# A gated recurrence on one core: the inner level of the input products is divided by pairs of PSUM quadrants

## The chip, the cores and the metric

The kernel runs on one core of one Trainium2 chip. The metric is device time in microseconds (us) for one execution of the whole program. Engines are named as in the profile: PE (TensorE matmul), PEld (its weight loads), DVE (VectorE), ACT (ScalarE), POOL (GpSimd), SP (SyncE, which issues the DMAs).

## What is computed

A gated recurrent layer runs over 512 time steps for a batch of 8, with 512 inputs and 512 hidden units in float32, and its states are added to the input:

```
fused = sigmoid(concat([x_t, h]) @ w_W + w_b)
hidden_state, output_state = split(fused, 2)
memory_state = x_t @ wx_W + wx_b + hidden_state * (h @ wh_W + wh_b)
h_new = output_state * h + (1 - output_state) * tanh(memory_state)
out = x + hs            # hs: all 512 states
```

Two kinds of matrix products occur. Those with `h` depend on the step before. Those with `x_t` do not, and can be made ahead for many steps at once.

## The kernel before

**Steps.** The loop over `i` goes through T = 512 steps. All engines follow an order written out by hand (`tc.manual_schedule()`). A chunk is TC = 16 steps, a group is GS = 4 steps (`g, s = divmod(i, GS)`), and w is the place of a step in its chunk (0 to 15).

In each step PE first makes the products with `h`, in the order `A0 A1 A2 A3 D0 D1 D2 D3 H2 H3`. The digit is the quarter k of the contraction, and each entry is four matmuls, one for each quadrant j of 32 PSUM partitions. A0 and A1 write 256 columns of bank A, A2 and A3 write 192, D 128, H 64. A0, A1 need the first half of the state (`hT[0]`), A2, A3 the second (`hT[1]`). A float32 matmul appears in the trace as two MATMUL records and two weight loads. All of them are recorded at line L196, the helper `mm`.

Behind these, PE gets some of the products with `x` for the chunk after this one (`take(later, 3)`, or 4 in the last step of a chunk).

DVE and ACT turn the sums of step i into the new state. In DVE's order: `tr`, `md1A` and `tz` are 32x32 block transposes out of bank A (L534, L549); two scans `m<-md0A,md1A` (L522, `memory(0, .)`) read the two SBUF tiles md0A and md1A; transposes of A, D and H; two scans `hT<-hd0A,hT` (`update(0, .)`, first half of the new state); two scans `m<-md0B,md1B`; two transposes of `sz`; two scans `hT<-hd0B,hT` (`update(1, .)`, second half). ACT makes the sigmoids and tanhs between them. Behind the last scan stand DVE's jobs that no state waits for: `drain` (L398), transposes of `xs` (`turn_x`, L292) and two small memsets. Then comes `tr` of the next step, which waits for PE's bank A.

POOL begins each step's work with `ot<-xin,hT` (L686), the sum of x and the new state, and then does the jobs that are listed for that step: `for job, *args in jobs.get(i, ())`.

**Products with x.** For chunks 2 to 31 they are made by a fast scheme with two levels: seven outer products p, each made of seven inner products q. The inner level goes through `STAGES = (2, 5, 3, 1, 6, 7, 4)`. In each stage the seven outer products lie in two PSUM banks (`xps`), three in bank 0 (288 columns) and four in bank 1 (384 columns). One unit of work is one outer product: four matmuls of 96 columns, one for each quadrant. That is 49 units a chunk: three a step, four in step 15. A `drain` adds a bank to a tile in SBUF: stages 2, 5, 3 into `ee`, stages 1, 6, 7, 4 into `ff`. There are 14 drains a chunk, at most one a step.

**POOL's jobs.** The operands for the fast scheme come from sums of x on POOL: `x_sums`, 16 jobs for each chunk, two a step at w = 3 to 10. The outer sums are `result(e, n)`, seven jobs of 192 columns for e = 0 (from `ff[0]`, listed from w = 11) and seven for e = 1 (from `ff[1]`, from w = 15), two a step:

```python
        for e, w in ((0, 11), (1, 15)):
            for m, n in enumerate((0, 3, 2, 4, 1, 5, 6)):
                at_step(w0 + w + m // 2, (result, e, n))
```

They write `xs[0..3]`, one for each group of four steps, from which ACT (`spread`) and DVE (`turn_x`) fill banks and operands one group ahead.

Of the kernel before, what the change touches and what calls it, by code (L numbers as in the profile page):

```python
# [46 lines left out]
COLS = slice(64, 448)  # L47
# [7 lines left out]
def tile_cond_rnn_residual(  # L55
# [38 lines left out]
    nc = tc.nc  # L94
# [4 lines left out]
    const = ctx.enter_context(tc.tile_pool(name="const", bufs=1))  # L99
# [11 lines left out]
    bias = head[:, :512]  # L111
# [21 lines left out]
    wx = const.tile([P, NQ, NQ, 384], F32, name="wx")  # L133
# [40 lines left out]
    idle = const.tile([P, IDLE], F32, name="idle")  # L174

    tw = const.tile([P, 4, 2, NQ, HALF], F32, name="tw")
    ti = const.tile([P, 7, 4, NQ, BL], F32, name="ti")
    so = [const.tile([P, 4, 2, 2, 32], F32, name=f"so{q}") for q in range(2)]
    si = [const.tile([P, 7, 4, 32], F32, name=f"si{q}") for q in range(2)]
    off = [const.tile([P, 7, BL], F32, name=f"off{b}") for b in range(2)]  # L180
    ee = [const.tile([P, 7, BL], F32, name=f"ee{n}") for n in range(3)]
    ff = [const.tile([P, 7, 2, BL], F32, name=f"ff{n}") for n in range(2)]
    xs = [const.tile([P, 576], F32, name=f"xs{n}") for n in range(4)]

    def state(hf, i, slot=2):
# [7 lines left out]
    xps = [psum.tile([P, 512], F32, name=f"xp{q}") for q in range(2)]  # L193

    def mm(out_, lhsT, rhs, start=False):
        nc.tensor.matmul(  # L196
            out_, lhsT, rhs, start=start, stop=False, skip_group_check=True
        )
# [32 lines left out]
    def wx_of(kh, nh):  # L231
        return wx[:, 2 * kh : 2 * kh + 2, :, HALF * nh : HALF * nh + HALF]
# [5 lines left out]
    for t_ in xs[1:] + xs[:1]:  # L238
        nc.gpsimd.tensor_copy(t_[:, 64:128], bias[:, :64])
        nc.gpsimd.tensor_copy(t_[:, 512:], bias[:, 448:])  # L240
    for b in range(2):
        c0 = COLS.start + BL * b
        nc.gpsimd.tensor_copy(off[b][:, 0], bias[:, c0 : c0 + BL])
        nc.gpsimd.tensor_tensor(
            off[b][:, 6], bias[:, c0 + HALF : c0 + HALF + BL], bias[:, c0 : c0 + BL], ALU.subtract
        )
    for hf in range(2):
        for slot in (0, 2):
# [45 lines left out]
    def inner_weight(n, p, j=slice(0, NQ)):  # L294

        def w(k, b):
            c0 = slice(BL * b, BL * b + BL)
            if p < 2:
                return wx[:, 2 * p + k, j, c0]
            if p == 2:  # L300
                return wx[:, 2 + k, j, HALF + BL * b : HALF + BL * b + BL]
            return tw[:, p - 3, k, j, c0]

        a, b = [
            (w(0, 1), w(0, 0)),
            (w(1, 1), ti[:, p, 0, j]),
            (w(1, 1), w(0, 1)),
            (w(1, 0), ti[:, p, 1, j]),
        ][n]
# [36 lines left out]
    def x_sums(c):  # L346
        jobs = [(x_sum, c, n) for n in range(4)]
        return jobs + [(inner_x, c, n, p) for n in range(4) for p in (0, 2, 3)]

    def left(c, p, q):  # L350

        xr, kh = {1: (0, 0), 2: (0, 1), 4: (1, 1)}.get(p, (None, None))
        at = {1: 0, 2: 1, 4: 2, 5: 3, 6: 4, 7: 5, 3: 6}[p]
        if q in (3, 5, 6, 7):
            return si[c % 2][:, at, {5: 0, 6: 1, 7: 2, 3: 3}[q]]
        e, k = {1: (0, 0), 2: (0, 1), 4: (1, 1)}[q]
        if xr is None:
            return so[c % 2][:, at - 3, e, k]
        return x_block(c, xr, kh)[:, e, k]

    def right(p, q, j):

        kh, nh = {1: (0, 0), 2: (1, 0), 3: (1, 1)}.get(p, (None, None))
# [4 lines left out]
        w = tw[:, at - 3] if kh is None else wx_of(kh, nh)  # L368
        return w[:, k, j, BL * b : BL * b + BL]

    def products(c):

        for q in STAGES:
            for bank in range(2):
                for n, p in enumerate(SLOTS[bank]):
                    for j in range(NQ):
                        mm(
                            xps[bank][32 * j : 32 * j + 32, BL * n : BL * n + BL],
                            left(c, p, q),
                            right(p, q, j),  # L380
                            start=q in FRESH and n == 0,
                        )
                    yield

    def drain(q, bank):

        at, n = (slice(0, 3), 3) if bank == 0 else (slice(3, 7), 4)
        to, with_ = {
            2: (ee[0], off[0]),
            5: (ee[1], off[1]),  # L390
            3: (ee[2], off[1]),
            1: (ff[0][:, :, 0], ee[0]),
            6: (ff[0][:, :, 1], ee[2]),
            7: (ff[1][:, :, 1], ee[1]),
            4: (ff[1][:, :, 0], off[0]),
        }[q]
        src = xps[bank][:, : BL * n].rearrange("p (n b) -> p n b", n=n)
        nc.vector.tensor_tensor(to[:, at], src, with_[:, at], ALU.add)  # L398

    def result(e, n):  # L400

        f = [ff[e][:, v].rearrange("p b c -> p (b c)") for v in range(7)]
# [10 lines left out]
        nc.gpsimd.tensor_tensor(to, a, b, ALU.add)  # L413
# [38 lines left out]
    def at_step(i, *todo):  # L452
        jobs.setdefault(i, []).extend(todo)

    halves = [(n, p, h) for n in (0, 2, 1, 3) for p in range(7) for h in range(2) if n or p > 4]
    for at in range(0, len(halves), 3):
        for n, p, h in halves[at : at + 3]:
            todo = late.setdefault(at // 3, [])
            if h and todo and todo[-1][:2] == (n, p):
                todo[-1] = (n, p, slice(0, 4))  # L460
            else:
                todo.append((n, p, slice(2 * h, 2 * h + 2)))
    drains = {}
    for c in range(2, NCH):
        w0 = TC * c - LEAD
        for n, q in enumerate(x_sums(c)):
            at_step(w0 - (13 if c > 2 else 10) + n // 2, q)
        done = 0
        for w in range(TC):
            n = done  # L470
            done += 3 + w // 15
            for m, q in enumerate(STAGES):
                for bank in range(2):
                    if n < 7 * m + 3 + 4 * bank <= done:
                        drains.setdefault(w0 + w, []).append((q, bank))
        for e, w in ((0, 11), (1, 15)):
            for m, n in enumerate((0, 3, 2, 4, 1, 5, 6)):
                at_step(w0 + w + m // 2, (result, e, n))

    pool_done = {}  # L480
    for i in range(T):
        g, s = divmod(i, GS)
        c, t = divmod(i, TC)
        ps = banks[g % 2]
        if c > 0 and t in (1, 4, 7, 10):
            e, k = divmod(t // 3, 2)
# [5 lines left out]
        for n in (ORDER if i else FIRST).split():  # L492
            if n == "x":
# [153 lines left out]
        for d in drains.get(i, ()):  # L647
            drain(*d)
# [121 lines left out]
```

## Time and profile before

| | |
|---|---|
| three runs | 1629.16, 1630.44, 1631.74 us (median 1630.44) |
| profiled execution | 1634.49 us, of which the profiled span is 1632.7 us |
| granted TensorE clock | 1.0 |
| PE busy | 1622.7 us (99% of the span) |
| DVE / ACT / POOL busy | 1411.5 (86%) / 977.0 (60%) / 541.9 us (33%) |
| MATMUL records | 53291 |

The median of the three runs is 4 us below the profiled execution. Busy PE time counts a matmul from its start to its modelled end, and matmuls overlap, so the 99% do not say that PE has no time to spare.

### The profile page before, as it was taken

How to read it: one execution, taken by the hardware profiler on the slowest of the kernel's cores; microseconds unless marked ns; L12 is line 12 of the kernel's file. 1: busy time of each engine (PE TensorE's matmuls, PEld its weight loads, DVE VectorE, ACT ScalarE, POOL GpSimd, SP SyncE). 2: the span in 40 equal slices, each digit the busy share in tenths (PEclk: the TensorE clock that was granted, in tenths of full speed). 3: DMA queues.
4: the chain of work that ended last, by engine and by line, in shares of the span. 5: the costliest groups of instructions: out<-in, count | busy, mean ns of one | idle time of the engine just before them, and what ended most of it. 6: DMA issues, size and time to landing. Idle time of an engine off the chain costs nothing.

```text
span 1632.7 us, 126805 instructions
## 1 busy us (share of the span) xinstructions
PE 1622.7 (99%) x53291; PEld 1372.3 (84%) x53291; DVE 1411.5 (86%) x11757; ACT 977.0 (60%) x5521; POOL 541.9 (33%) x1443
## 2 busy tenths in 40 slices
PE   9999999999999999999999999999999999999998
PEld 6888888888888888888888888888888888888886
DVE  8988888888888888888888888888888888888887
ACT  4665666656666666566556566666665666665665
POOL 2333333333333333333333333333333333333320
PEclk9999999999999999999999999999999999999999
DMA  4000000000000000000000000000000000000000
GB/s 191 12 14 18 16 14 13 18 15 16 15 18 13 15 16 17 15 13 14 18 16 15 13 17 15 16 15 18 13 15 16 18 15 13 15 18 10 10 10 10
DMA packets 37437, 31.47 MB, mean 19 GB/s; under 512 B 4096, under 2 KB 35200, under 8 KB 36864
## 3 DMA queue, kind: packets, MB, share of 16 engines
q1 hardware_dynamic: 36864, 23.36, 4.6%
q8 instruction: 416, 6.82, 1.7%
q14 instruction: 157, 1.29, 0.3%
HBM read 14.96 MB, written 8.39 MB: 14 GB/s over the span
## 4 chain that ended last, share of the span: by engine, by line
PE 98%; DVE 1%; issue 0%; DVEq 0%
PE A L196 49%; PE D L196 27%; PE xp L196 16%; PE H L196 7%; DVE tr L534 0%; DVE m L522 0%; DVE md1B L592 0%; DVE hT L522 0%; DVE md1A L549 0%; DVE tz L534 0%; DVE md1B L549 0%; DVE zeros L163 0%; DVE hd0B L585 0%; DVE idle L557 0%; DVE ot L667 0%
## 5 line engine op out<-in xcount | busy, mean ns | idle before, releaser
L196 PE MATMUL A<-wa,hT 128*32 128x256 f32 x16352 | 882.5, 355 | 4.1 <-DVE hT L522 4.0
L196 PEld LDWEIGHTS A<-wa,hT 128*32 128x32 f32 x16352 | 512.0, 123 | 223.2 <-DVE hT L522 127.7
L196 PE MATMUL D<-wd,hT 128*32 128x128 f32 x16384 | 544.9, 273 | 0.0
L196 PEld LDWEIGHTS D<-wd,hT 128*32 128x32 f32 x16384 | 485.2, 122 | 19.6 <-DMA wd<-in_wd_dram 0.2
L686 POOL TENSOR_TENSOR ot<-xin,hT 128x32 f32<-128x32 f32 x503 | 134.5, 267 | 1041.7 <-DVE hT L522 957.8
L258 ACT ACTIVATE hT<-m 128x8 f32<-128x8 f32 x2048 | 323.9, 207 | 94.5 <-DVE m L522 93.7
L258 ACT ACTIVATE md0A<-tr 128x16 f32<-128x16 f32 x512 | 112.9, 221 | 389.9 <-DVE tr L534 389.9
L534 DVE STREAM_TRANSPOSE tr<-A 128x64 f32<-128x64 f32 x511 | 127.7, 250 | 205.4 <-PE A L196 204.7
L258 ACT ACTIVATE hT<-hT 128x16 f32<-128x16 f32 x1024 | 232.2, 227 | 92.0 <-DVE hT L522 85.3
L196 PE MATMUL H<-wa,hT 128*32 128x64 f32 x8208 | 212.3, 219 | 0.0
L196 PEld LDWEIGHTS H<-wa,hT 128*32 128x32 f32 x8208 | 189.6, 122 | 0.0
L522 DVE TENSOR_TENSOR_SCAN hT<-hd0A,hT 128x24 f32<-128x24 f32 x1024 | 172.7, 169 | 0.0
L522 DVE TENSOR_TENSOR_SCAN hT<-hd0B,hT 128x24 f32<-128x24 f32 x1024 | 171.9, 208 | 0.8 <-DVE hT L522 0.8
L522 DVE TENSOR_TENSOR_SCAN m<-md0B,md1B 128x24 f32<-128x24 f32 x1024 | 154.7, 193 | 0.4 <-issue 0.4
L196 PE MATMUL xp<-ti,si 128*32 128x96 f32 x5040 | 150.6, 246 | 0.0
L585 DVE STREAM_TRANSPOSE hd0B<-sz 128x32 f32<-128x32 f32 x1024 | 149.1, 191 | 0.0
L522 DVE TENSOR_TENSOR_SCAN m<-md0A,md1A 128x16 f32<-128x16 f32 x1024 | 143.8, 182 | 5.0
L413 POOL TENSOR_TENSOR xs<-ff 128x192 f32<-128x192 f32 x240 | 140.8, 597 | 4.7
L258 ACT ACTIVATE md0B<-tr 128x16 f32<-128x16 f32 x512 | 116.3, 227 | 41.8 <-DVE tr L534 1.2
L592 DVE STREAM_TRANSPOSE md1B<-A 128x64 f32<-128x64 f32 x511 | 130.0, 254 | 0.0
L258 ACT ACTIVATE hd0A<-tz 128x16 f32<-128x16 f32 x512 | 116.4, 227 | 21.5
L549 DVE STREAM_TRANSPOSE md1B<-H 128x64 f32<-128x64 f32 x512 | 128.3, 251 | 0.0
(109 smaller groups left out, 1906.0 us busy)
## 6 DMA issues: line engine op xcount, KB each, us to landing
out_dram<-ot SPq DMA_DIRECT2D x128, 64.0 KB, 1.7
xin<-in_x_dram SPq DMA_DIRECT2D x112, 64.0 KB, 2.5
wx<-in_wx_dram SPq DMA_DIRECT2D x4, 768.0 KB, 7.9
wa<-in_wa_dram SPq DMA_DIRECT2D x4, 512.0 KB, 11.5
wd<-in_wd_dram SPq DMA_DIRECT2D x1, 768.0 KB, 11.4
xin<-in_x_dram SPq DMA_DIRECT2D x2, 256.0 KB, 8.2
head<-in_xh_dram SPq DMA_DIRECT2D x1, 400.0 KB, 3.0
xin<-in_x_dram SPq DMA_DIRECT2D x3, 128.0 KB, 8.7
```

The costliest lines, as they stand in the source:

```text
L196: nc.tensor.matmul(out_, lhsT, rhs, start=start, stop=False, skip_group_check=True)
L258: inst = nc.scalar.activation(out_, in_, func, **kw).ins
L413: nc.gpsimd.tensor_tensor(to, a, b, ALU.add)
L522: return nc.vector.tensor_tensor_scan(*[t_[:, :, c_].rearrange("p n c s -> p (n c s)") for t_ in (out_, d0, d1)], 0.0, ALU.mult, ALU.add,).ins
L534: inst = nc.vector.transpose(t_.rearrange("p c n -> p (c n)"), raw[n][hf]).ins
L549: inst = nc.vector.transpose(md1[hf][g % 2][:, :, :, hf].rearrange("p n c -> p c n"), raw["h"][hf]).ins
L585: nc.vector.transpose(hd0[1][i % 2][:, :, q, 2], sz[:, 32 * q : 32 * q + 32]).ins
L592: nc.vector.transpose(md1[1][g % 2][:, :, :, 0].rearrange("p n c -> p c n"), ps["A"][:, :HU])
L686: pool_done[i + 1] = nc.gpsimd.tensor_tensor(ot[:, t], x_of(c, slice(0, NQ), t, 1), hTs[(i + 1) % NH][:, :, :, B * s1 : B * s1 + B, 2].rea ...
```

## The change

In a stage, the seven outer products no longer take one column block each over all four quadrants. Two products now share 192 columns: one uses quadrants 0 and 1, the other quadrants 2 and 3 (`PASS`). Passes A, B (bank 0, now 384 columns) and C (bank 1, now 288 columns) hold two products each. Pass D holds the seventh alone, 96 columns wide. A unit is still four matmuls of 96 columns, but `deal` hands PE as many units of one pass as it still may in this step, in one group of four matmuls. A step with three units becomes two groups (192 and 96 columns), 8 matmuls in place of 12; the step with four units becomes two groups of 192.

The halves of a result now lie in different quadrants from where they are needed. For stages 1, 6, 7 and 4, `drain` is followed by DMAs on SP that move 64 partitions: one for each bank after stages 1 and 7, two for each bank after stages 6 and 4, which go by way of a new tile `tt`. That is 12 DMAs a chunk of 64 x 384 or 64 x 288 float32.

The drains stand at other steps: (stage, bank) (2,0) moves from w = 0 to 1, (1,0) from 7 to 8, and stage 4 has bank 1 at w = 14 and bank 0 at 15; the others stay at their steps. The seven `result` jobs for e = 0 begin at w = 12, three a step (3, 3, 1). Those for e = 1 begin one step later than before, at w = 0 of the next chunk, two a step (2, 2, 2, 1), so that the last falls on w = 3. The order of the seven is now 2, 0, 3, 4, 1, 5, 6.

The weights' sums (`inner_weight`) and the offsets (`off`) are laid out anew in the same number of elements. The core of the diff:

```diff
-SLOTS = ((1, 6, 7), (2, 3, 4, 5))
+ORDERS = ("ABCD", "ABDC", "ABCD", "ABCD", "ABDC", "ABCD", "CDAB")
+PASS = {
+    "A": (0, ((1, 0, 0), (3, 0, 0)), HALF),
+    "B": (0, ((5, HALF, 0), (4, HALF, 0)), HALF),
+    "C": (1, ((6, 0, 0), (2, BL, 0)), HALF),
+    "D": (1, ((7, HALF, 0), (7, 0, BL)), BL),
+}
+WIDE = (384, 288)
+FCOL = (0, 384, 576, 768, 960, 1152, 192)
+PIECE = (((0, 384), (384, 672)), ((960, 1344), (672, 960)))
...
     def products(c):
-        for q in STAGES:
-            for bank in range(2):
-                for n, p in enumerate(SLOTS[bank]):
-                    for j in range(NQ):
-                        mm(
-                            xps[bank][32 * j : 32 * j + 32, BL * n : BL * n + BL],
-                            left(c, p, q),
-                            right(p, q, j),
-                            start=q in FRESH and n == 0,
-                        )
-                    yield
+        fresh = set()
+        for q, order in zip(STAGES, ORDERS):
+            if q in FRESH:
+                fresh = {0, 1}
+            for name in order:
+                bank, sides, w = PASS[name]
+                at = 0
+                while at < w:
+                    n = yield
+                    to = min(w, at + BL * n)
+                    for h, (p, c0, w0) in enumerate(sides):
+                        for j in range(2):
+                            r0 = 64 * h + 32 * j
+                            mm(
+                                xps[bank][r0 : r0 + 32, c0 + at : c0 + to],
+                                left(c, p, q),
+                                right(p, q, j)[:, w0 + at : w0 + to],
+                                start=bank in fresh,
+                            )
+                    fresh.discard(bank)
+                    yield (to - at) // BL
+                    at = to

     def drain(q, bank):
...
+        at = slice(0, 384) if bank == 0 else slice(384, 672)
+        e, b = {1: (0, 0), 6: (0, 1), 7: (1, 1), 4: (1, 0)}.get(q, (0, 0))
+        own, moved = (slice(*PIECE[h][bank]) for h in (b, 1 - b))
+        here, there = (slice(64 * h, 64 * h + 64) for h in (b, 1 - b))
+        with_ = {2: off[0], 5: off[1], 3: off[1], 1: ee[0], 6: ee[2], 7: ee[1], 4: off[0]}[q]
+        to = {2: ee[0], 5: ee[1], 3: ee[2], 6: tt, 4: tt}.get(q)
+        to = ff[e][:, own] if to is None else to[:, at]
+        nc.vector.tensor_tensor(to, xps[bank][:, : WIDE[bank]], with_[:, at], ALU.add)
+        if q in (6, 4):
+            nc.sync.dma_start(out=ff[e][here, own], in_=to[here])
+        if q in (1, 6, 7, 4):
+            nc.sync.dma_start(out=ff[e][here, moved], in_=to[there])
...
+    def deal(it, n):
+        while n > 0 and next(it, it) is None:
+            n -= it.send(n)
...
-        for e, w in ((0, 11), (1, 15)):
-            for m, n in enumerate((0, 3, 2, 4, 1, 5, 6)):
-                at_step(w0 + w + m // 2, (result, e, n))
+        unit = 0
+        for q, order in zip(STAGES, ORDERS):
+            for name in order:
+                unit += PASS[name][2] // BL
+                if name in (order[1], order[3]):
+                    w = min((unit - 1) // 3, TC - 1)
+                    drains.setdefault(w0 + w, []).append((q, PASS[name][0]))
+        for e, w, n in ((0, 12, 3), (1, 16, 2)):
+            for m, job in enumerate((2, 0, 3, 4, 1, 5, 6)):
+                at_step(w0 + w + m // n, (result, e, job))
...
-            take(later, 4 if (i + LEAD) % TC == TC - 1 else 3)
+            deal(later, 4 if (i + LEAD) % TC == TC - 1 else 3)
```

More of the change, by code (lines that the diff above doesn't have):

```diff
@@ L176, in tile_cond_rnn_residual @@
     tw = const.tile([P, 4, 2, NQ, HALF], F32, name="tw")
-    ti = const.tile([P, 7, 4, NQ, BL], F32, name="ti")
+    ti = const.tile([P, 7, 4, 2, HALF], F32, name="ti")
     so = [const.tile([P, 4, 2, 2, 32], F32, name=f"so{q}") for q in range(2)]
     si = [const.tile([P, 7, 4, 32], F32, name=f"si{q}") for q in range(2)]
-    off = [const.tile([P, 7, BL], F32, name=f"off{b}") for b in range(2)]
-    ee = [const.tile([P, 7, BL], F32, name=f"ee{n}") for n in range(3)]
-    ff = [const.tile([P, 7, 2, BL], F32, name=f"ff{n}") for n in range(2)]
+    off = [const.tile([P, 7 * BL], F32, name=f"off{b}") for b in range(2)]
+    ee = [const.tile([P, 7 * BL], F32, name=f"ee{n}") for n in range(3)]
+    ff = [const.tile([P, 7 * HALF], F32, name=f"ff{n}") for n in range(2)]
+    tt = const.tile([P, 7 * BL], F32, name="tt")
     xs = [const.tile([P, 576], F32, name=f"xs{n}") for n in range(4)]
@@ L240, in tile_cond_rnn_residual @@
         nc.gpsimd.tensor_copy(t_[:, 512:], bias[:, 448:])
+    c0 = COLS.start
     for b in range(2):
-        c0 = COLS.start + BL * b
-        nc.gpsimd.tensor_copy(off[b][:, 0], bias[:, c0 : c0 + BL])
+        rows = slice(64 * b, 64 * b + 64)
+        nc.gpsimd.tensor_copy(off[b][:64, :HALF], bias[rows, c0 : c0 + HALF])
         nc.gpsimd.tensor_tensor(
-            off[b][:, 6], bias[:, c0 + HALF : c0 + HALF + BL], bias[:, c0 : c0 + BL], ALU.subtract
+            off[b][:64, HALF : 2 * HALF],
+            bias[rows, c0 + HALF : c0 + 2 * HALF],
+            bias[rows, c0 : c0 + HALF],
+            ALU.subtract,
         )
@@ L292, in turn_x, with block, inner_weight @@
         nc.vector.transpose(md1[e // 2][g % 2][:, :, e % 2, 1 + e // 2], source(g, c0, c0 + 32))
[L294 to L302, printed above, removed]
+    def block(at, k, b, j=slice(0, 2)):
+        j = slice(2 * b + j.start, 2 * b + j.stop)
+        if at < 2:
+            return wx[:, 2 * at + k, j, :HALF]
+        if at == 2:
+            return wx[:, 2 + k, j, HALF:]
+        return tw[:, at - 3, k, j]
+    def inner_weight(n, p, j=slice(0, 2)):
         a, b = [
[L305 to L308, printed above, removed]
+            (block(p, 0, 1, j), block(p, 0, 0, j)),
+            (block(p, 1, 1, j), ti[:, p, 0, j]),
+            (block(p, 1, 1, j), block(p, 0, 1, j)),
+            (block(p, 1, 0, j), ti[:, p, 1, j]),
         ][n]
@@ L361, in right @@
     def right(p, q, j):
-        kh, nh = {1: (0, 0), 2: (1, 0), 3: (1, 1)}.get(p, (None, None))
         at = {1: 0, 2: 1, 3: 2, 5: 3, 6: 4, 7: 5, 4: 6}[p]
@@ L367, in right @@
         k, b = {1: (0, 0), 2: (1, 0), 3: (1, 1)}[q]
-        w = tw[:, at - 3] if kh is None else wx_of(kh, nh)
-        return w[:, k, j, BL * b : BL * b + BL]
+        return block(at, k, b)[:, j]
     def products(c):
-        for q in STAGES:
-            for bank in range(2):
-                for n, p in enumerate(SLOTS[bank]):
-                    for j in range(NQ):
-                        mm(
-                            xps[bank][32 * j : 32 * j + 32, BL * n : BL * n + BL],
-                            left(c, p, q),
-                            right(p, q, j),
-                            start=q in FRESH and n == 0,
-                        )
-                    yield
@@ L385, in drain @@
-    def drain(q, bank):
[L387 to L398, printed above, removed]
+        fresh = set()
@@ L400, in result @@
     def result(e, n):
-        f = [ff[e][:, v].rearrange("p b c -> p (b c)") for v in range(7)]
+        f = [ff[e][:, v : v + HALF] for v in FCOL]
         y = [[xs[2 * e + r][:, SC.start + HALF * v : SC.start + HALF * v + HALF] for v in range(2)] for r in range(2)]
@@ L459, in tile_cond_rnn_residual @@
             if h and todo and todo[-1][:2] == (n, p):
-                todo[-1] = (n, p, slice(0, 4))
+                todo[-1] = (n, p, slice(0, 2))
             else:
-                todo.append((n, p, slice(2 * h, 2 * h + 2)))
+                todo.append((n, p, slice(h, h + 1)))
     drains = {}
@@ L467, in tile_cond_rnn_residual @@
             at_step(w0 - (13 if c > 2 else 10) + n // 2, q)
[L468 to L475, printed above, removed]
-        for e, w in ((0, 11), (1, 15)):
-            for m, n in enumerate((0, 3, 2, 4, 1, 5, 6)):
-                at_step(w0 + w + m // 2, (result, e, n))
+        unit = 0
[8 more added lines that the diff above has]
+                at_step(w0 + w + m // n, (result, e, job))
     pool_done = {}
```

## The prediction

> **What bounds the kernel now.** I read the engines' busy time first, then the waits, the distance between two steps, and PE's timeline where it has least to do.
>
> ```profile
> PE 1622.7 (99%) x53291; PEld 1372.3 (84%) x53291; DVE 1411.5 (86%) x11757; ACT 977.0 (60%) x5521; POOL 541.9 (33%) x1443
> ```
>
> By this PE is full, and fewer matmuls should shorten the kernel. The waits say otherwise (us in total, times, longest):
>
> ```profile
> PEld A L196 <- DVE hT L522: 127.7, 478, 0.8
> DVE tr L534 <- PE A L196: 204.7, 493, 1.3
> ```
>
> In nearly every step PE's weight load for A waits for the new state, 127.7/478 = 0.27 us, and DVE's first transpose waits for bank A, 204.7/493 = 0.42 us. So there is a ring: bank A ends, DVE and ACT make the second half of the state, A2 and A3 use it, bank A ends. D, H, the x products, A0 and A1 lie beside the ring. The transposes `tz`, one a step, test this. The first row covers steps 480 to 495, the second the last sixteen, in which no x products are left:
>
> ```profile
> L534 DVE STREAM_TRANSPOSE tz<-A x16: 207/208/211, 1531.1 to 1577.9; 128x64 f32<-128x64 f32 x16
> L534 DVE STREAM_TRANSPOSE tz<-A x16: 207/208/210, 1581.2 to 1628.0; 128x64 f32<-128x64 f32 x16
> ```
>
> (1577.9 - 1531.1)/15 = 3.12 us a step with x products, (1628.0 - 1581.2)/15 = 3.12 us without. PE's timeline shows both kinds of step:
>
> ```profile
> 775.79 1.06 PE L196 MATMUL D<-wd,hT 128*32 128x128 f32 x32
> 776.67 0.41 PE L196 MATMUL H<-wa,hT 128*32 128x64 f32 x16
> 776.89 0.35 PE L196 MATMUL xp<-wx,xin 128*32 128x96 f32 x8
> ...
> 777.38 1.71 PE L196 MATMUL A<-wa,hT 128*32 128x256 f32 x32
> ...
> 1603.93 1.78 PE L196 MATMUL A<-wa,hT 128*32 128x256 f32 x32 [0.24 <-DVE hT L522]
> ```
>
> The x products take from 776.89 to 777.38, 0.49 us. In a step without them PE stands 0.24 us ahead of A, waiting for hT, and the step is as long as ever. They fill a hole. What sets the step is the ring, and most of the ring is DVE.
>
> **What DVE shares with POOL.** Here is POOL over four steps. Each begins with `ot`, then come the step's jobs:
>
> ```profile
> 1230.86 0.27 POOL L686 TENSOR_TENSOR ot<-xin,hT 128x32 f32<-128x32 f32 x1 [1.91 <-DVE hT L522]
> 1231.08 1.16 POOL L413 TENSOR_TENSOR xs<-ff 128x192 f32<-128x192 f32 x2
> 1234.34 0.26 POOL L686 TENSOR_TENSOR ot<-xin,hT 128x32 f32<-128x32 f32 x1 [2.10 <-DVE hT L522]
> 1234.56 0.60 POOL L413 TENSOR_TENSOR ff<-ff 128x192 f32<-128x192 f32 x1
> 1235.24 0.60 POOL L413 TENSOR_TENSOR xs<-ff 128x192 f32<-128x192 f32 x1
> 1237.48 0.26 POOL L686 TENSOR_TENSOR ot<-xin,hT 128x32 f32<-128x32 f32 x1 [1.65 <-DVE hT L522]
> ...
> 1240.81 0.46 POOL L325 TENSOR_TENSOR so<-xin 128x128 f32<-128x128 f32 x1
> ```
>
> And DVE over the same time, then the first scan `m` of two steps by itself (ns min/median/max):
>
> ```profile
> 1231.96 0.21 DVE L534 STREAM_TRANSPOSE tz<-A 128x64 f32<-128x64 f32 x1
> 1232.19 0.28 DVE L522 TENSOR_TENSOR_SCAN m<-md0A,md1A 128x16 f32<-128x16 f32 x2
> 1232.70 0.17 DVE L522 TENSOR_TENSOR_SCAN hT<-hd0A,hT 128x24 f32<-128x24 f32 x1
> ...
> 1235.23 0.21 DVE L534 STREAM_TRANSPOSE tz<-A 128x64 f32<-128x64 f32 x1
> 1235.47 0.50 DVE L522 TENSOR_TENSOR_SCAN m<-md0A,md1A 128x16 f32<-128x16 f32 x2
> ...
> 1237.32 0.53 DVE L398 TENSOR_TENSOR ee<-xp,off 128x384 f32<-128x384 f32 x1
> ...
> 1238.27 0.25 DVE L534 STREAM_TRANSPOSE tr<-A 128x64 f32<-128x64 f32 x1 [0.27 <-PE A L196]
> ...
> 1238.57 0.21 DVE L534 STREAM_TRANSPOSE tz<-A 128x64 f32<-128x64 f32 x1
> ```
> ```profile
> L522 DVE TENSOR_TENSOR_SCAN m<-md0A,md1A x1: 416/416/416, 1235.5 to 1235.5; 128x16 f32<-128x16 f32 x1
> L522 DVE TENSOR_TENSOR_SCAN m<-md0A,md1A x1: 193/193/193, 1238.8 to 1238.8; 128x16 f32<-128x16 f32 x1
> ```
>
> At 1232.19 the two jobs are ending (1231.08 + 1.16 = 1232.24) and the scans take their usual 0.28. At 1235.47 a job of POOL still runs until 1235.24 + 0.60 = 1235.84. The first scan takes 416 ns in place of 193 and ends at 1235.89, 0.05 after the job. The step pays all of it: 1238.57 - 1235.23 = 3.34 us, 0.22 over 3.12, and 416 - 193 is 0.22. The same once more, elsewhere:
>
> ```profile
> 813.71 1.15 POOL L413 TENSOR_TENSOR ff<-ff 128x192 f32<-128x192 f32 x2
> ```
> ```profile
> L522 DVE TENSOR_TENSOR_SCAN m<-md0A,md1A x1: 291/291/291, 814.6 to 814.6; 128x16 f32<-128x16 f32 x1
> ```
> ```profile
> 814.62 0.38 DVE L522 TENSOR_TENSOR_SCAN m<-md0A,md1A 128x16 f32<-128x16 f32 x2
> ```
>
> The pair ends at 814.86, the scan at 814.62 + 0.29 = 814.91, again 0.05 later. So a scan with two SBUF inputs doesn't run slower beside a job of POOL: it stands until the job is over. Two jobs of 192 columns just fit ahead of the first scan.
>
> **The change part by part.**
>
> *PE.* Each step has one group of four matmuls less (32 groups in place of 49 a chunk) at the same number of columns. A group runs as two sets of four records. D has eight sets of 128 columns in 0.88 us (775.79 to 776.67), 110 ns each; H has four of 64 in 0.22, 55 ns each. Half the columns take half the time: a fixed part of a set doesn't show. With 0.01 us of rounding on each, 2 x 57.5 - 109 = 6 ns is its upper end, and two sets a group make at most 17 x 30 x 0.012 = 6.1 us of PE time, 0 at the lower end. Fifteen steps of sixteen are set by the ring, so that drops out of the time; only the step with four units, where PE may be last, can keep its two groups of those 17, 0.7 us at most. I take 0.3. The Trainium skill, in "TensorE: Matmul & The Clock Gate" ("Wait — 56ns, not 53.3ns?"), gives about 2.5 ns of fixed cost for each matmul. By it the 34 sets a chunk would be worth 2.6 us of PE time, inside these bounds and as well hidden.
>
> *Drains.* Their widths are swapped between the banks, with the same total. In the rows above DVE still has 0.27 us idle after a 384-column drain (0.53 us) and a turn of `xs`, before `tr` gets bank A. No step has two drains. PE uses a drained bank again one step later at the earliest. Cost 0; if that cover were gone, each step would pay what goes beyond 0.27.
>
> *DMAs.* SP's queue has little in it:
>
> ```profile
> 1240.88 0.33 SPq L677 DMA_DIRECT2D out_dram<-ot  x1
> ```
> ```profile
> out_dram<-ot SPq DMA_DIRECT2D x128, 64.0 KB, 1.7
> xin<-in_x_dram SPq DMA_DIRECT2D x112, 64.0 KB, 2.5
> ```
>
> A move inside SBUF isn't in this trace; these two are its bounds, 1.7 and 2.5 us. The last drain for e = 0 starts 0.16 us before its step's `ot` (1237.32 against 1237.48). With 0.53 us for it and two issues of 0.33 both moves are under way 1.03 us after `ot` starts, and land at 2.7 to 3.5. The first job of the next step is due 3.12 + 0.22 = 3.34 after that `ot`. So POOL gets its data between 0.6 us early and 0.2 late; I take early. Stores queued behind the moves have nobody waiting for them. The results feed ACT's `spread` at the end of the following step, so late ones have about 2 us before ACT stands.
>
> *POOL's jobs.* This is the costly part. In the changed program's instruction order, no step of a chunk before has more than two jobs behind its `ot`. After the change there are three at w = 12 and 13 (30 chunks) and at w = 3 (28 chunks: the last result meets two of the x sums). I put them on the clock of the step that starts with `ot` at 1230.86, where the first scan ends at 1232.19 + 0.19 = 1232.38 and the second at 1232.47.
> - w = 12: a job more adds 1.16 - 0.60 = 0.56, to 1232.80. The scan ends at 1232.85: +0.47.
> - w = 13: the third job needs the second's result. Such a pair has a gap of 0.08 (1234.56 + 0.60 to 1235.24), so the third begins at 1232.32 and ends at 1232.92. The first scan gets by, the second ends at 1232.97: +0.50. If it holds the first, +0.59.
> - w = 3: 0.60, 0.42, a gap of 0.08 and 0.46 end at 1232.64; the last of the three starts at 1232.18, just ahead of the scan. The scan ends at 1232.69: +0.31.
>
> 30 x 0.47 + 30 x 0.50 + 28 x 0.31 = 37.8 us. The Trainium skill agrees with the rows on the wait: "SBUF — State Buffer" ("SBUF: two separate sides") has DVE instructions with two SBUF inputs and POOL instructions that read SBUF share a port pair, held by whichever starts first for a whole instruction. By that rule the first scan, issued at 1232.19, would go ahead of the third job at w = 12, and the second would stand until about 1232.92 instead: +0.45, for a sum of 37 us.
>
> **Sum.** 37.8 - 0.3 = +37.5 us. On the profiled execution's 1634.49 us that is 1672.0. The runs shown have a median 4 us lower, and against that it is 1667.9 us. Own range of this forecast: 1655 to 1675.
>
> **Rivals.**
> - *The scans slip in between the jobs* (0.12). If DVE wins every handover, both scans pass and only `hT<-hd0A` stands, which ends at 1232.87. The third job then runs from 1232.47 to 1233.03, so +0.2 at w = 12 and 13 and at most +0.1 at w = 3: 12 to 15 us, 1645. For it: a scan may be waiting when a job ends. Against: nothing here shows POOL standing for DVE.
> - *The moves land late* (0.08). If POOL gets its data 0.3 late, w = 12 costs 0.3 more and the pair at w = 0 ends at 1232.54, holding the scan until 1232.59, +0.21: 30 x 0.51 = 15 us more, 1683.
> - *Faster: PE's groups come through* (0.05). It decides if the ring isn't what sets the step and POOL's third job meets no scan. Half of the upper end, 3 us, gives 1627.4. Against it stand the sixteen last steps.
> - *Nothing moves* (0.03): the third jobs harmless and PE hidden, 1630.
>
> **How the numbers follow.** The forecast has 0.72. With 0.12 and 0.08 that makes 0.92 for slower by over 0.2% (3.3 us, about what a measurement of this kernel can tell from no change). "Faster" has 0.03 of its rival's 0.05, within 0.2% the other 0.02 and the 0.03. The range goes from the low rival to the high one, 1645 to 1683.
>
> **What would show it.** In the profile after: first or second scans `m<-md0A,md1A` of 0.4 to 0.7 us in three steps of sixteen, ending 0.05 after a job of POOL; those steps 3.4 to 3.6 us long, the others 3.12; the wait of PE for hT up by 30 to 40 us. It is wrong if the steps behind w = 12, 13 and 3 stay at 3.12, or if other steps grow.

## The result, and the profile after

The changed kernel takes **1655.2 us** (median of 4 runs, 1654.6 to 1656.6), the kernel before 1630.8 (4 runs, 1629.2 to 1631.7): a ratio of 1.0152 with a 95% interval of 1.0134 to 1.0169. That is slower by 24.4 us. The prediction had 1667.9 with a range of 1645 to 1683, and a chance of 0.92 for slower; the time lies at the lower edge of the forecast's own range, 1655 to 1675. The profiled execution of the changed kernel took 1655.01 us, its span was 1653.2 us and the granted clock 1.0, as before.

I read the views in the order of the prediction. First the engines' busy time:

```profile
PE 1636.7 (99%) x49211; PEld 1311.3 (79%) x49211; DVE 1440.5 (87%) x11757; ACT 978.7 (59%) x5521; POOL 545.4 (33%) x1443
```

PE has 4080 records less (53291 before), and is "busy" for 14 us more: that figure follows the span and says nothing of what PE could do. POOL has as many instructions as before (1443) and about the same busy time. Then the two waits of the ring:

```profile
DVE tr L566 <- PE A L210: 195.3, 491, 0.9
PEld A L210 <- DVE hT L554: 163.1, 582, 0.8
```

DVE's wait for bank A is nearly as before (204.7). PE's wait for the new state rose from 127.7 to 163.1 us, by 35. So PE gives back nothing, it stands longer: the ring got longer on the side of DVE and ACT. The last sixteen steps (the first row) still take (1648.7 - 1601.8)/15 = 3.13 us. The sixteen ahead of them (the second row) take (1598.6 - 1551.2)/15 = 3.16:

```profile
L566 DVE STREAM_TRANSPOSE tz<-A x16: 205/208/210, 1601.8 to 1648.7; 128x64 f32<-128x64 f32 x16
L566 DVE STREAM_TRANSPOSE tz<-A x16: 207/208/209, 1551.2 to 1598.6; 128x64 f32<-128x64 f32 x16
```

They are longer by 0.6 us than before in all, and 0.43 of it is one single step of 3.55 us. The distance from each `tz` to the next, taken from the trace for steps 32 to 479 and sorted by the place of the step in its chunk, shows where the time went. These are medians over 28 chunks in ns, worked out from the starts of all `tz`; a place that isn't listed differs by at most 5 ns. "Behind w" is the step in which the jobs listed for w meet the scans.

| step | before | after | change |
|---|---|---|---|
| behind w = 12 | 3122 | 3565 | +443 |
| behind w = 13 | 3140 | 3226 | +86 |
| behind w = 3 | 3117 | 3411 (mean 3400) | +294 (by that mean +283) |
| behind w = 1 and w = 2 | 3137, 3119 | 3148, 3147 | +11, +28 |
| the steps w = 1 and w = 8 themselves | 3123, 3118 | 3154, 3151 | +31, +33 |
| w = 15 (four units) | 3271 | 3260 | -11 |

Now the three places one by one. POOL in the steps that begin at w = 12 and w = 13 of one chunk:

```profile
570.68 0.27 POOL L718 TENSOR_TENSOR ot<-xin,hT 128x32 f32<-128x32 f32 x1 [2.85 <-DVE hT L554]
570.90 0.59 POOL L441 TENSOR_TENSOR xs<-ff 128x192 f32<-128x192 f32 x1
571.46 1.15 POOL L441 TENSOR_TENSOR ff<-ff 128x192 f32<-128x192 f32 x2
574.25 0.26 POOL L718 TENSOR_TENSOR ot<-xin,hT 128x32 f32<-128x32 f32 x1 [1.63 <-DVE hT L554]
574.47 0.59 POOL L441 TENSOR_TENSOR xs<-ff 128x192 f32<-128x192 f32 x1
575.02 0.59 POOL L441 TENSOR_TENSOR ff<-ff 128x192 f32<-128x192 f32 x1
575.69 0.61 POOL L441 TENSOR_TENSOR xs<-ff 128x192 f32<-128x192 f32 x1
```

DVE over the same time, then by itself the first scan behind w = 12, both scans behind w = 13, and the first half-state scan behind w = 13 (ns min/median/max):

```profile
571.77 0.21 DVE L566 STREAM_TRANSPOSE tz<-A 128x64 f32<-128x64 f32 x1
572.01 0.73 DVE L554 TENSOR_TENSOR_SCAN m<-md0A,md1A 128x16 f32<-128x16 f32 x2
...
575.34 0.21 DVE L566 STREAM_TRANSPOSE tz<-A 128x64 f32<-128x64 f32 x1
575.58 0.28 DVE L554 TENSOR_TENSOR_SCAN m<-md0A,md1A 128x16 f32<-128x16 f32 x2
```
```profile
L554 DVE TENSOR_TENSOR_SCAN m<-md0A,md1A x1: 649/649/649, 572.0 to 572.0; 128x16 f32<-128x16 f32 x1
L554 DVE TENSOR_TENSOR_SCAN m<-md0A,md1A x2: 171/182/192, 575.6 to 575.7; 128x16 f32<-128x16 f32 x2
L554 DVE TENSOR_TENSOR_SCAN hT<-hd0A,hT x1: 285/285/285, 576.1 to 576.1; 128x24 f32<-128x24 f32 x1
```

*Behind w = 12.* POOL's three jobs end at 571.46 + 1.15 = 572.61. The scan that starts at 572.01 takes 649 ns in place of 193 and ends at 572.66, 0.05 later. It stands for the whole third job.

*Behind w = 13.* The third job begins at 575.69, after the gap that its dependence makes (575.02 + 0.59 = 575.61, so 0.08). The two scans are already under way, at 575.58 and about 0.01 ahead of the job, and take their usual 192 and 171. What stands is the next scan with two SBUF inputs, `hT<-hd0A`: 285 ns, until 576.09 + 0.285 = 576.37, 0.07 behind the job's end at 576.30. The step pays only 0.09.

*Behind w = 3.* Here the third job starts within a few ns of the scan:

```profile
543.18 0.46 POOL L344 TENSOR_TENSOR so<-xin 128x128 f32<-128x128 f32 x1
543.72 0.50 POOL L344 TENSOR_TENSOR so<-so,xin 128x128 f32<-128x128 f32 x1
```
```profile
L554 DVE TENSOR_TENSOR_SCAN m<-md0A,md1A x2: 192/318/443, 543.7 to 543.8; 128x16 f32<-128x16 f32 x2
```

In this chunk the first scan gets by (192 ns) and the second stands (443 ns, until 544.28; the job ends at 544.22): +0.22. In most chunks the first scan loses (499 ns): the 28 steps fall into 8 of 3339 to 3350 ns and 20 of 3391 or more. In the 8 the job starts 0 to 6 ns ahead of the first scan, in the 20 it starts 6 to 27 ns ahead. POOL stands too: where the first scan gets by, its third job takes 500 to 510 ns, else 457 to 464.

What POOL needs from the new DMAs is there in time. Their rows among the DMA issues, and POOL's only waits for them:

```profile
ff<-tt SPq DMA_DIRECT2D x120, 96.0 KB, 2.1
ff<-tt SPq DMA_DIRECT2D x120, 72.0 KB, 2.0
```
```profile
POOL ff L441 <- DMA ff<-tt: 0.6, 1, 0.6
POOL xs L441 <- DMA ff<-tt: 0.5, 2, 0.3
```

### The profile page after: what moved, and what is told of

It is laid out like the page before. It is cut to its first block, busy times and chain, and to the rows that moved or that the text cites. A ratio compares the mean times of both kernels' runs of the same rounds, so it can differ in the third digit from the quotient of the medians.

```text
span 1653.2 us, 119515 instructions
## 1 busy us (share of the span) xinstructions
PE 1636.7 (99%) x49211; PEld 1311.3 (79%) x49211; DVE 1440.5 (87%) x11757; ACT 978.7 (59%) x5521; POOL 545.4 (33%) x1443
## 4 chain that ended last, share of the span: by engine, by line
PE 93%; DVE 6%; issue 0%; DMA 0%; SPq 0%; ACT 0%
PE A L210 49%; PE D L210 24%; PE xp L210 14%; PE H L210 6%; DVE m L554 2%; DVE tr L566 1%; DVE md1B L624 1%; DVE hT L554 1%; DVE md1A L581 1%; DVE tz L566 1%; DMA wx<-in_wx_dram 0%; DVE idle L589 0%; DVE hd0B L617 0%; DVE ee L422 0%; DVE md1B L581 0%
## 5 line engine op out<-in xcount | busy, mean ns | idle before, releaser
L210 PEld LDWEIGHTS A<-wa,hT 128*32 128x32 f32 x16352 | 495.6, 124 | 285.8 <-DVE hT L554 163.1
L566 DVE STREAM_TRANSPOSE tr<-A 128x64 f32<-128x64 f32 x511 | 127.7, 250 | 196.1 <-PE A L210 195.3
L210 PE MATMUL H<-wa,hT 128*32 128x64 f32 x8208 | 208.3, 219 | 0.0
L210 PEld LDWEIGHTS H<-wa,hT 128*32 128x32 f32 x8208 | 185.9, 122 | 0.0
L554 DVE TENSOR_TENSOR_SCAN hT<-hd0A,hT 128x24 f32<-128x24 f32 x1024 | 178.3, 174 | 0.0
L554 DVE TENSOR_TENSOR_SCAN m<-md0A,md1A 128x16 f32<-128x16 f32 x1024 | 165.2, 202 | 4.9
L210 PE MATMUL xp<-ti,si 128*32 128x192 f32 (+1 forms) x3120 | 146.7, 295 | 0.0
```

The lines of the kernel that those rows point to most:

```text
L210: nc.tensor.matmul(out_, lhsT, rhs, start=start, stop=False, skip_group_check=True)
L554: return nc.vector.tensor_tensor_scan(*[t_[:, :, c_].rearrange("p n c s -> p (n c s)") for t_ in (out_, d0, d1)], 0.0, ALU.mult, ALU.add,).ins
L566: inst = nc.vector.transpose(t_.rearrange("p c n -> p (c n)"), raw[n][hf]).ins
```

## The experiments

**Without the third jobs.** `e1_two` is the changed kernel with its groups, drains and moves, and at most two POOL jobs a step.

```diff
-            at_step(w0 - (13 if c > 2 else 10) + n // 2, q)
+            at_step(w0 - (12 if c > 2 else 10) + n // 2, q)
...
-        for e, w, n in ((0, 12, 3), (1, 16, 2)):
+        for e, w, n in ((0, 12, 2), (1, 16, 2)):
```

> The changed kernel with at most two POOL jobs a step: the results for e = 0 two a step from w = 12, the x sums one step later. All else of the change stays (groups, moves, drains). If the third jobs hold DVE's scans, the traces before and after give their price as means of the steps: 0.43 us at w = 13, 0.09 at 14, 0.26 at 4, so 30 x 0.52 + 28 x 0.26 = 23 us go, and the kernel is within 2.5 us of the one before (1629 to 1634 us), its first scans all under 0.25 us. If the moves or the new groups cost the time, it stays within 3 us of 1655.

Measured: 1632.96 us, ratio 1.0014 (1.0004 to 1.0023). The steps behind w = 12 and w = 3 are at 3120 and 3114 ns, the one behind w = 13 at 3142. PE's wait for the state is down to this:

```profile
PEld A L210 <- DVE hT L554: 144.6, 533, 0.8
```

22 of the 24 us go with the third jobs alone. PE's groups, all still there, bring nothing against the kernel before.

**Only the third jobs.** `e2_before_three` is the kernel before, with one group per product and no moves, and only the result jobs listed as in the changed kernel.

```diff
-        for e, w in ((0, 11), (1, 15)):
-            for m, n in enumerate((0, 3, 2, 4, 1, 5, 6)):
-                at_step(w0 + w + m // 2, (result, e, n))
+        for e, w, n in ((0, 12, 3), (1, 16, 2)):
+            for m, job in enumerate((2, 0, 3, 4, 1, 5, 6)):
+                at_step(w0 + w + m // n, (result, e, job))
```

> The kernel before with one part of the change alone: its result jobs at the changed kernel's steps and in its order (three a step at w = 12 and 13, the last one at w = 3 beside two x sums). No new groups, no moves. If the third jobs are the cause: 20 to 26 us slower than before (1651 to 1657 us). If the moves or the groups are: no change, 1629 to 1633.

Measured: 1654.28 us, ratio 1.0146 (1.0129 to 1.0163), so 23.6 us of the 24.4. The same three steps grow by the same amounts: 3565, 3230 and 3414 ns. The rows of the POOL pair and the scan behind w = 12 are those of the changed kernel over again:

```profile
571.46 1.15 POOL L413 TENSOR_TENSOR ff<-ff 128x192 f32<-128x192 f32 x2
```
```profile
L522 DVE TENSOR_TENSOR_SCAN m<-md0A,md1A x1: 641/641/641, 572.0 to 572.0; 128x16 f32<-128x16 f32 x1
```

From both sides: the cost is POOL's list of jobs, not PE, the drains or the moves.

**Is it POOL's reading?** `e4_fill` is the kernel before with one more POOL job at w = 12 and 13 that only writes: a memset of 128x608, as long as a sum.

```diff
+    spare = const.tile([P, 608], F32, name="spare")
+    def fill():
+        nc.gpsimd.memset(spare, 0.0)
...
+        for w in (12, 13):
+            at_step(w0 + w, (fill,))
```

> The kernel before with a third POOL job added at w = 12 and 13 that only writes: a memset of 608 columns, about 0.6 us as the two memsets of 672 columns took 0.66. If it is enough that POOL is busy, this costs what the third results cost, 0.43 + 0.09 us a chunk or more: 14 to 28 us. If POOL must read SBUF beside a scan with two SBUF inputs (the Trainium skill, SBUF — State Buffer, Who interferes with whom), it costs nothing: within 1.5 us of before.

Measured: 1630.63 us, ratio 1.0001 (0.9992 to 1.0010). POOL and DVE behind w = 12:

```profile
563.91 1.15 POOL L413 TENSOR_TENSOR xs<-ff 128x192 f32<-128x192 f32 x2
565.00 0.61 POOL L419 MEMSET spare<- 128x608 f32 x1
```
```profile
565.02 0.28 DVE L530 TENSOR_TENSOR_SCAN m<-md0A,md1A 128x16 f32<-128x16 f32 x2
```

The memset runs from 565.00 to 565.61, right over the two scans, and they take their usual 0.28. So a busy POOL isn't what holds the scan. The jobs that held it in the other runs read SBUF, and this one only writes. That is the condition which the Trainium skill states in "SBUF — State Buffer" ("SBUF: two separate sides"): two SBUF inputs on DVE contend only with a POOL instruction that reads SBUF.

**The groups alone.** `e3_ungrouped` is `e1_two` with groups of 96 columns only, so twelve matmuls a step again.

```diff
-            n -= it.send(n)
+            n -= it.send(1)
```

> The kernel with two POOL jobs a step, but PE's groups undone: never more than 96 columns in a group of four matmuls, 12 matmuls a step as before the change. If the ring of DVE and bank A sets the step, 17 more groups a chunk cost nothing but in the step with four units: 0 to 0.7 us more than the same kernel with groups. If PE sets the step, a set's fixed part (the traces have 82.5 ns for sets of 96 columns, 162.5 for 192, so 2.5 ns) makes it 17 x 2 x 30 x 2.5 ns = 2.6 us slower, and up to 6 us by the upper end.

Measured: 1640.16 us, ratio 1.0056 (1.0041 to 1.0071): 7.2 us above `e1_two`, more than either reading allowed. The usual steps don't differ: their medians over the chunk sum to 1504.9 us for 480 steps, in `e1_two` to 1505.5. The time is in irregular ones. 43 steps are over 30 ns above the median of their place, 7.1 us together (in `e1_two` 10, 1.4 us), 23 of them at w = 1 and w = 13. There POOL starts late because a move hasn't landed:

```profile
POOL ff L441 <- DMA ff<-tt: 4.2, 6, 1.0
POOL xs L441 <- DMA ff<-tt: 3.7, 10, 0.7
```

So the groups do bring something, by a way that the expectation doesn't have: with them, POOL's waits for the moves are 0.5 us in all, without them 7.9. The medians of issue to landing differ little (2.1 and 2.0 us with, 2.2 and 2.2 without). They aren't issued later either: the last move of the first end is issued 2.91 us after `tz` in both. But it takes 2.31 us in place of 2.01 (medians), and at most 3.98 in place of 3.13. Why these transfers take longer without the groups isn't settled.

**What a late move costs.** `e5_moves_twice` is `e1_two` with each move issued twice.

```diff
         if q in (6, 4):
-            nc.sync.dma_start(out=ff[e][here, own], in_=to[here])
+            for _ in range(2):
+                nc.sync.dma_start(out=ff[e][here, own], in_=to[here])
         if q in (1, 6, 7, 4):
-            nc.sync.dma_start(out=ff[e][here, moved], in_=to[there])
+            for _ in range(2):
+                nc.sync.dma_start(out=ff[e][here, moved], in_=to[there])
```

> The kernel with two POOL jobs a step, each of the 12 moves a chunk issued twice. If the moves cost nothing but where they land late, POOL's first job at w = 12 and w = 0 waits more often (two or three times in 28 chunks before, now in most), and each late start pushes the pair over the first scan: up to 0.5 us for each, 5 to 25 us more than 1633. If landing has room to spare: within 1 us of 1633. If the queue itself slowed the engines, all steps would grow, not those behind w = 12 and w = 0 alone.

Measured: 1895.62, 1897.94 and 1920.57 us, ratio 1.1666 (1.1603 to 1.1728); a fourth execution took 3265.1 us and isn't in the ratio. It isn't the clean doubling it was meant to be. The second copy writes the same place, so SP waits until the first has landed; the moves became a chain of twice the time, and POOL and then the step stand for it:

```profile
SPq L425 <- DMA ff<-tt: 274.9, 120, 3.7
```
```profile
POOL xs L443 <- DMA ff<-tt: 399.3, 50, 11.1
ACT A L305 <- POOL xs L443: 191.5, 30, 8.7
```

Only the steps at w = 3 to 5 and 13 to 15 grow (9.6 us in place of 3.1 at w = 13). In the changed kernel the moves lie just ahead of that: they are free, with little to spare.

**The order of the jobs in the kernel before.** In the table above the steps w = 2 and w = 14 of the kernel before are 0.02 us longer than the rest (3137, 3140): there the second job of a step needs the first one's result. `e7_before_order` parts such pairs.

```diff
-            for m, n in enumerate((0, 3, 2, 4, 1, 5, 6)):
-                at_step(w0 + w + m // 2, (result, e, n))
+            for m, todo in enumerate(((0, 3), (2, 4), (1,), (5, 6))):
+                at_step(w0 + w + m, *[(result, e, n) for n in todo])
```

> The kernel before, its result jobs as (0, 3), (2, 4), (1), (5, 6) over the same four steps, so that no job follows one whose result it needs. The pair with the gap of 0.08 us now ends 0.05 us past the point where the first scan stands (steps w = 2 and 14 are 3.137 and 3.140 us against 3.118). If the port is what holds the scan, both steps fall to 3.118 to 3.123: 1.0 to 1.3 us faster in all, 1629.5. If the gap isn't the cause: no change.

Measured: 1631.70 us, the kernel before beside it 1632.87, ratio 0.9993 (0.9984 to 1.0002). Both steps fell to 3117 as expected, worth 1.2 us; in the whole time that can't be told from no change.

**Splitting by columns.** `e8_columns` is `e7_before_order` with 294 columns of x products in every step, cut at any column, so that no step has four units.

```diff
+COLUMNS = 294
...
-            take(later, 4 if (i + LEAD) % TC == TC - 1 else 3)
+            deal(later, COLUMNS)
```

> The kernel before with that job order, and the 49th unit of a chunk spread: PE gets 294 columns of the x products in every step, in place of 288 and once 384. The step with four units (3.271 us) is the one that PE sets, 0.153 us over the ring; it goes. 294 columns in about four pieces a step make PE's own step 2.61 + 0.49 + 0.02 = 3.12 us, level with the ring. If the ring sets the step: 15 steps gain 0 to 0.006, one loses 0.15, so 30 x (0.153 - 0.06) + 1.2 = 2 to 5.5 us faster than before, 1625 to 1629. If PE sets all steps, the same columns in more pieces cost more: 1631 or slower.

Measured: 1696.62 us, ratio 1.0393 (1.0378 to 1.0408), far from the 1625 to 1629 that were expected. The cuts leave sets of 6 to 90 columns, and 3600 records more (56891). In a product of 6 to 36 columns the second set of four records starts 37 to 57 ns behind the first (medians), where 6 columns at the pace of the wide sets (216 ns for 256) would take 5. The x products of a step are spread over 0.50 to 0.69 us in place of 0.43, and the weight loads stand idle without a wait that the profile shows ("issue"):

```profile
PEld xp L198 <- issue: 28.4, 80, 1.0
```

DVE's part of the step is as long as before: its last scan ends 1.94 to 1.95 us after `tz`, as in `e7_before_order`. But the last A set starts up to 0.43 us later, in the step behind w = 4. So PE can become late after all, by many small sets rather than by columns. The Trainium skill's "TensorE: Matmul & The Clock Gate" ("Wait — 56ns, not 53.3ns?") states a floor of about 25 ns from one matmul's start to the next. The small sets here stay above it.

**The same with groups.** `e6_best` has the changed kernel's groups and moves, two POOL jobs a step, and 288 or 296 columns a step, with the order of the passes changed to suit.

```diff
+COLUMNS = 4 * (288,) + 12 * (296,)
+RESULTS = (((2, 0), (3, 4), (1,), (5, 6)), ((0, 3), (2, 4), (1,), (5, 6)))
```

> The changed kernel's groups and moves, two POOL jobs a step, one pair with a gap left, and the 49th unit spread: 288 columns in four steps, 296 in twelve, in 2.5 groups a step. PE's own step is 2.61 + 0.50 = 3.11 us, under the ring everywhere. By the ring: the four-unit step gives 0.14 us, the pairs at w = 2 and 3 0.05, two steps keep their 0.03: 30 x 0.19 = 5.7 us under the kernel with two jobs a step, about 1627. If the late moves weigh (w = 12 and w = 0), up to 5 us of that is lost.

Measured: 1638.5 us, ratio 1.0033 (1.0020 to 1.0046). The four-unit step went from 3260 to 3117 ns as meant, and the pairs' steps are at 3117 and 3121. But bank 0 is now drained after step 11, its moves land behind POOL's turn, and the steps w = 13 (3381) and w = 1 (3238 on the mean) give back more than that:

```profile
POOL xs L445 <- DMA ff<-tt: 10.4, 13, 1.5
POOL ff L445 <- DMA ff<-tt: 5.8, 10, 0.9
```

**The gaps inside pairs.** `e9_pairs` and `e10_orders` start from `e1_two`. Both list the results as below; the second also puts pass D ahead of C in stages 2 and 1. My list moved the sum 2 for e = 0 behind the copies that read it, so these copies take the sums of the chunk before.

```diff
+            for m, todo in enumerate(((3, 0), (2, 4), (1,), (5, 6))):
+                at_step(w0 + w + m, *[(result, e, job) for job in todo])
```

> The changed kernel with its groups, widths, drains and moves, at most two POOL jobs a step as in e1_two, and the seven results of both ends in the turns (3, 0), (2, 4), (1), (5, 6), so that no job of a turn needs the result of the one ahead of it. In e1_two three steps of a chunk are longer by the gap inside a pair: w = 2 and w = 3 take 3150 and 3149 ns, w = 14 3142. If the gap holds the first scan there, all three go to 3117, worth (0.033 + 0.032 + 0.025) x 30 = 2.7 us, and the time is about that of the kernel before (1630). w = 1 and w = 8 stay at 3150. The first turn needs less of the moved data (3: bank 0 alone), so POOL starts no later than in e1_two. If those steps are long for another reason (the moved halves, the drains), they stay where they are and the time is that of e1_two, 0.14% above before.

> e9_pairs with the pass D ahead of C in stages 2 and 1, as two other stages have it. In every grouped kernel so far, and never in the kernel before, the steps w = 1 and w = 8 take 3150 ns, because the transpose of H takes 290 ns in place of 250 there. These are the two steps in which the x products are 96 columns of pass B and then 192 of pass C, and the bank is drained in the same step. With D ahead of C the 96 columns are followed by two groups of 96. If the wide group behind the 96 columns is what lengthens the transpose, both steps fall to 3117: 0.033 x 56 = 1.9 us less than e9_pairs, about 1628.5. If it is the drained bank itself (its last group and its signal), both stay at 3150 and the time is that of e9_pairs. The columns and the drains keep their steps in both.

Measured: 1638.48 us (1.0049, 1.0035 to 1.0062) and 1641.77 (1.0066, 1.0054 to 1.0079). The steps w = 2 and w = 3 fell to between 3117 and 3121 in both, as the gap theory has it. Two other things ate it. The misplaced sum waits for ACT's copies, which makes w = 14 3347 ns on the mean in `e9_pairs`. And job 3 at the head of the turn needs the last move of all; in ten of 29 chunks POOL began it 0.1 to 0.8 us late, and w = 1 is 3218 on the mean (waits of `e9_pairs`):

```profile
POOL xs L441 <- ACT A L305: 8.2, 30, 0.3
POOL ot L718 <- DMA ff<-tt: 5.7, 3, 1.9
POOL ff L441 <- DMA ff<-tt: 2.5, 7, 0.6
```

In `e10_orders` w = 1 and w = 8 are at 3142 and 3136 (medians), so neither at the 3117 nor at the 3150 of its two readings.

`e11_turns` mends both: (2, 0), (3, 4), (1), (5, 6) for the first end and (2, 0), (3), (4, 1), (5, 6) for the second.

> e1_two with the results for the second end in the turns (2, 0), (3), (4, 1), (5, 6): no job needs the one ahead of it in its turn, the first turn needs nothing of the last move, and each sum stands ahead of its readers. For the first end (2, 0), (3, 4), (1), (5, 6): 4 has to follow 3 at w = 13, so one gap stays. By the gap theory w = 2 and w = 3 fall from 3150 to 3117, w = 14 stays at 3142, and w = 1 has none of the late starts of e9_pairs (where 3, which needs the last move, stood first): 0.065 x 30 = 2.0 us less than e1_two, about 1631, within 0.1% of before. If the late starts came from the gapless turns as such, w = 1 is 3.2 us or more on the mean again.

Measured: 1631.65 us, the kernel before beside it 1632.13, ratio 0.9996 (0.9987 to 1.0005). On the mean w = 2 and w = 3 are at 3121 and 3117, w = 1 at 3155. The division by pairs of quadrants, with its moves, then costs nothing and brings nothing.

Neither this version nor `e7_before_order` can be told from the kernel before; no version here is faster.

## Why the prediction was right, and where its sum was off

**Ring, not PE: right.** 4080 matmul records less moved nothing. Even the small fixed cost is visible and hidden: from the last H to the first A, PE takes 526 ns in place of 531 (medians of the starts), 5 ns for one group less, against the bound of 12 ns. Over 480 steps that is 2.4 us of PE's time, close to the 2.6 by the 2.5 ns a matmul of the Trainium skill's "TensorE: Matmul & The Clock Gate" ("Wait — 56ns, not 53.3ns?"). The four-unit step gained 11 ns, 0.3 us, as predicted.

**w = 12: right.** Predicted +0.47, measured +0.44: 30 x 0.443 = 13.3 us against 14.1. That it is the first scan that stands was luck: apart from three chunks in which POOL began late, it starts between 14 ns behind the third job and 18 ns ahead of it. In one chunk it passes, 18 ns ahead, and the second scan stands for 580 ns; that step takes 3.48 us, so the price is much the same. What the sum doesn't allow for is a scan that waits for one job and then goes first. In one of those three chunks the scan had been standing for 0.35 us when the third job started:

```profile
368.08 1.18 POOL L441 TENSOR_TENSOR ff<-ff 128x192 f32<-128x192 f32 x2
```
```profile
L554 DVE TENSOR_TENSOR_SCAN m<-md0A,md1A x1: 433/433/433, 368.3 to 368.3; 128x16 f32<-128x16 f32 x1
```

It starts at 368.28, so it ends at 368.71. The second job ends at about 368.67 and the third at 369.26: the scan went in between, as in the first rival, and the third job took 0.62 us in place of 0.60. The last section has all such cases.

**w = 13: the term that was mis-sized.** Predicted +0.50, measured +0.09: 2.6 us in place of 15.0. The clock was right: the third job begins 0.35 us after `tz`, predicted 0.36. The second scan starts 0.34 after it, so it was ahead, and an instruction that has begun isn't held. By the prediction's own numbers the second scan, which ends at 1232.47 and takes some 0.17, begins at 1232.30, just ahead of the job at 1232.32; it let the job hold it all the same. Its own rival, the scans that pass and `hT<-hd0A` that stands, is what happened at this place, though the rival had it for all three places and priced it at 0.2. The reason given against it, nothing shows POOL standing for DVE, missed the point: at w = 13 POOL needn't stand, and at w = 3 and in the chunk above it does. By the rule that the prediction quotes, whoever starts first keeps the port, this could have been read off.

**w = 3: right.** Predicted +0.31, measured +0.28 on the mean: 7.9 us against 8.7. The prediction saw the two starts as close; they are a tie that mostly goes to POOL.

**Not foreseen.** Four small steps, w = 1 and w = 8 (+0.03 each) and the ones behind w = 1 and w = 2 (+0.01, +0.03): 3.1 us in all. The last two are the gap inside a pair, whose 0.08 the prediction used at w = 13 but not here; `e11_turns` shows it by taking them away. For the first two, see below. "The others 3.12" was wrong by this much.

**Drains, moves: right, with less margin than it seems.** POOL's waits for the moves are 1.1 us in all, as "early" had it. `e3_ungrouped`, `e6_best` and `e9_pairs` show how near the other case was.

The sum of the terms as measured is 13.3 + 2.6 + 7.9 + 3.1 - 0.3 = 26.6 us, against 24.4 by the medians of the runs; the 2 us between them I can't place. Of the 13 us by which the forecast was high, w = 13 is 12.4. The two profiled executions differ by 20.5 us only, because the one of before holds 31 steps of over 30 ns above the median of their place (5.2 us), the one of after 5 (0.8 us).

## What to carry to other kernels

Before you count matmuls, look for steps without the work you would speed up: if they are as long as the others, the work fills a hole. When you move jobs between engines' lists, put every start on one clock, and ask of each neighbour on a shared port which of the two has begun first; 10 ns decided between 0.50 and 0.09 us here. Jobs on a side engine cost nothing until one more of them reaches into the ring's own instruction, and then the whole overlap is paid in every pass.

## What the runs showed of the hardware

- When one POOL job follows directly on another, a waiting scan can go in between. The 13 traces have 88 such handovers between sums, in which a scan starts ahead of the second job and isn't over when that starts. In all 29 in which it starts 1 to 13 ns ahead, it stands for the second job; of the 6 at 18 to 23 ns, 4 do. In none of the 53 at 36 ns and more does it. The 48 of these at 139 ns and more end 45 to 66 ns behind the end of the first job. The other 5, at 36 to 101 ns, take their usual 191 or 192 ns, so the first job doesn't hold them in the last stretch of its record. So whoever starts first does go first, but the recorded starts tell that only to some 20 ns: at w = 12 the scan shown starts 6 ns ahead of the third job (234 and 240 ns after `tz`) and loses. The scan's record counts its standing too.
- A POOL memset doesn't hold the scans (`e4_fill`).
- In the changed kernel the transpose `md1B<-H` takes 290 ns in place of 250 in the steps w = 1 and w = 8, in 20 and 23 of 28 chunks, and that is their +0.03. Here at w = 7, 8 and 9 of one chunk:

```profile
L581 DVE STREAM_TRANSPOSE md1B<-H x1: 250/250/250, 604.8 to 604.8; 128x64 f32<-128x64 f32 x1
L581 DVE STREAM_TRANSPOSE md1B<-H x1: 290/290/290, 607.9 to 607.9; 128x64 f32<-128x64 f32 x1
L581 DVE STREAM_TRANSPOSE md1B<-H x1: 251/251/251, 611.1 to 611.1; 128x64 f32<-128x64 f32 x1
```

  These are the steps in which 96 columns end a bank and 192 columns of the other bank follow. Without groups it is 256 and 267 ns (`e3_ungrouped`, medians), with the 192 columns parted 254 and 271 (`e10_orders`). So the wide group behind the end of a bank has to do with it, though at w = 8 some 20 ns stay without it; by what way stays open.
